# The third weight combination of a chained convolution kernel, with 18 products instead of 19

## The chip, the cores and the metric

The kernel runs on one core of one Trainium2 chip. The metric is the device time of one execution in microseconds (us). TensorE is called PE (its weight loads PEld), VectorE DVE, ScalarE ACT, GpSimd POOL, and SyncE SP. Each engine works through its own queue in the order in which the program issues to it.

## The reference

The input x has 128 samples of 64 channels by 1024 positions. Four layers follow each other, and the result is added to x. Each layer scales a 64x64x3 weight by a style vector of the sample, normalizes it (demodulation), and convolves.

```python
TYPES = ('same', 'upsample', 'same', 'downsample')
def _layer(x, style, w, b, mw, mb, typ):
    s = style @ mw.T + mb
    weight = SCALE * w * s[:, None, :, None]
    demod = lax.rsqrt(jnp.sum(weight * weight, axis=(2, 3)) + EPS)
    weight = weight * demod[:, :, None, None]
    # same: conv; upsample: transposed conv, then blur; downsample: blur, then strided conv
...
x = x + out
```

Nothing nonlinear stands between the layers, so for one sample the whole chain is one linear filter along the positions: nine taps of 64x64 numbers.

## The kernel before, in words

All data are 32-bit floats. The 128 samples are worked on in 32 groups q of four. A group is held as two pairs; a pair has one sample on the upper and one on the lower 64 partitions. Every matmul uses a 64x64 quarter of the PE array, and the four quarters work side by side, so one "product" of a weight with a 64-column block stands in the profile as eight matmul records (two records for each of four quarters).

For each group the kernel first combines the four layers' weights into the nine taps, in three stages, and then filters x with them.

- `stage1_a` and `stage1_b` combine layers 3 and 2 into S (PE into the PSUM buffer psS, ACT evicts psS to S, DVE and POOL finish S). Matmuls L389.
- `stage2` combines S with the blurred layer 1 (E) into the seven blocks of R. Two of its contributions are computed ahead (`share`) and put under its PSUM buffer psR by an ACT copy (`share_copy`, L490). ACT evicts psR to R with two instructions (L545, L360 in the profile). Matmuls L467.
- `stage3` combines R with layer 0 (`woi[0]`) into the nine blocks of W, the third weight combination. In groups 6 to 30 it is split in two. `stage3_b` accumulates twelve products in spare room of a buffer psA, and ACT makes of them two things: four copies psW<-psA of the shared part, and five evicted blocks Wf<-psA. `stage3_a` adds seven products on top of the copies in psW, and ACT evicts four blocks Wf<-psW. Matmuls L571. One POOL instruction (`r_sums`, L588) first adds two pairs of blocks of R, for the shared products.

W is kept with three kinds of taps, and these carry the factors 1, 1/3 and -2. Before the change the factors stand in scaled copies `w0s` of the layer-0 weight, and each kind's three taps lie on their own places (`TAPS`).

The filtering uses five products m = 0..4 of three steps each (`product`, L753, 24 records of 340 columns a product): `conv3`, `conv1`, `conv2` and `conv0` go into psA, `conv4` into the buffer Y. Between them DVE reads psA and prepares what follows: `sum1` (y<-psA,m), `sum2` (two instructions Y<-m,psA, one for each bank of Y, then y<-y,psA). `conv4` adds to Y what it finds there, so it comes after both Y<-m,psA. `combine_a` and `combine_b` (DVE, H<-Wf) make the weights of products 1 to 3. ACT writes the outputs (o<-...), SP loads x and stores the results.

The order is written out by hand (`tc.manual_schedule()`). The loop `turn_of(q)` runs for q = 4 to 28 (25 turns); the first, q = 4, is an `entry` with a slightly different order. With n = q+1, c = q+2, s = q+4, PE's order in a turn is: stage2(c), conv2(q), stage3_b(c), conv4(q), stage3_a(c), conv3(n), stage1_a(s), conv0(q), stage1_b(s), share(c+1), conv1(n). ACT's order is: evict R(c), the psW copies and Wf blocks of stage3_b, the Wf blocks of stage3_a, outputs(q, 2) from Y, evict S(s), copy_m3(n) (m<-psA), outputs(q, 1), share_copy(c+1), outputs(q, 0), scale3. The PSUM buffers psR, psW and psS take turns in the same two banks (pool `ps_w`, one buffer), so each has to be evicted before PE starts the next.

Of the kernel before, what the change touches and what calls it, by code (L numbers as in the profile page):

```python
# [48 lines left out]
F32 = mybir.dt.float32  # L49
# [5 lines left out]
C = 64  # L55
K = 3
# [7 lines left out]
def kernel(  # L64
# [12 lines left out]
    NQ = B // 4  # L77
# [186 lines left out]
    def var_newton(bs, ls=slice(0, NL)):  # L264
# [2 lines left out]


    ALT, ODD, DOWN = slice(0, 4, 2), slice(1, 4, 2), (slice(3, 4), slice(1, 2))
    tA, tB, tBn, tC, t0, t3, td, tb = (  # L270
        const.tile([P, NQ, 2], F32, name=n) for n in ("tA", "tB", "tBn", "tC", "t0", "t3", "td", "tb")
    )

    def table(eng, t, bs, upper, lower, src, mul):
# [24 lines left out]

    def table_0(bs):  # L300
        table(nc_g, t0, bs, ALT, ODD, sc[:, 0, bs], 1.0)


    def table_C(bs, eng=nc_g):
# [81 lines left out]
    def tap_matmul(ps, wd, at, n, weight, taps, first=False, last=False):  # L386
        for r, rows in enumerate(HALF):
            for c, cols in enumerate(HALF):
                nc.tensor.matmul(  # L389
                    ps[r][cols, at * C : (at + n) * C],  # L390
                    weight[rows],
                    wd[c if r == 0 else 1 - c][rows, taps],
                    start=first,
                    stop=last,
                    skip_group_check=True,
                )
# [5 lines left out]
    def flat(t):  # L402
        return t.rearrange("c a o -> c (a o)")
# [18 lines left out]
    def stage1_a(q, ps=None):  # L422

        ps = ps or unit(ps_w, f"psS{q}")
        wd = chain[q]
        tap_matmul(ps, wd, 2, 2, w2n[:, 0, :], EVEN, first=True)
        tap_matmul(ps, wd, 3, 2, w2n[:, 2, :], EVEN)
        tap_matmul(ps, wd, 1, 1, w2n[:, 1, :], slice(1, 2))
        st, t = s_tiles(q)
        for r in range(2):  # L430
            scaled_copy(nc_a, flat(st[r][:, :4]), ps[r][:, C : 5 * C], tBn[:, q, r : r + 1])
        chain[q] = wd, ps, st, t

    def stage1_b(q):

        wd, ps, st, t = chain[q]
        tap_matmul(ps, wd, 2, 1, w2n[:, 3, :], slice(3, 4))
        tap_matmul(ps, wd, 4, 1, w2n[:, 4, :], slice(4, 5), last=True)
        for r in range(2):
            p1 = st[r][:, 0:1, :].to_broadcast([P, 2, C])  # L440
            sums = ps[r][:, 2 * C : 6 * C].rearrange("c (a b o) -> c a b o", a=2, b=2)[:, :, 0]
            nc_v.scalar_tensor_tensor(
                st[r][:, 4:6, :], sums, tB[:, q, r : r + 1], p1, op0=ALU.mult, op1=ALU.subtract
            )
        nc_g.tensor_add(t[:, :, 2], t[:, :, 2], t[:, :, 0])  # L445
        chain[q] = st
        whole[q] = t
# [37 lines left out]
    def share_copy(q):  # L485

        ps = unit(ps_w, f"psR{q}")
        for r in range(2):
            src = shared_ps[q][r].rearrange("c (a o) -> c a o", a=2)
            nc_a.copy(  # L490
                ps[r][:, C : 5 * C].rearrange("c (a b o) -> c a b o", a=2, b=2),
                src[:, :, None, :].to_broadcast([P, 2, 2, C]),
            )
        shared_ps[q] = ps

    def stage2_rest(q):

        ps = shared_ps.pop(q)
        block = lambda i, n=1: [b[:, i * C : (i + n) * C] for b in ps]
        apart = [b[:, : 4 * C].rearrange("c (a b o) -> c a b o", a=2, b=2)[:, :, 0] for b in ps]  # L500
        plan = (
            (apart, E[:, 0], slice(1, 4, 2)),
            (block(1), Ed[:, 0], slice(2, 3)),
            (block(2), Ed[:, 1], slice(1, 2)),
            (block(3), E[:, 2], slice(3, 4)),
            (block(3), Ed[:, 2], slice(2, 3)),
            (block(4), Ed[:, 3], slice(1, 2)),
            (block(4), E[:, 4], slice(3, 4)),
            (block(5, 2), E[:, 8], slice(2, 4)),
            (block(5), E[:, 6], slice(3, 4)),  # L510
            (block(1, 2), E[:, 1], slice(4, 6)),
            (block(2), E[:, 3], slice(4, 5)),
            (block(3), Ed[:, 4], slice(5, 6)),
            (block(4), Ed[:, 5], slice(4, 5)),
            (block(5), E[:, 7], slice(5, 6)),
        )
        for n, (dst, weight, slots) in enumerate(plan):
            chain_matmul(dst, weight, chain[q], slots, n == len(plan) - 1)
        return ps

    def stage2(q, pool=None, engs=(nc_a, nc_a), between=None):
        st = chain[q]
        shared = q in shared_ps
        ps = stage2_rest(q) if shared else unit(pool or ps_w, f"psR{q}")
        for n, e in enumerate(() if shared else (-2, -1, 0, 1, 2, 3, 4, 5, 6)):
            if e % 2 == 0:
                a, lo, m = slice(1, 4), e // 2 + 1, 3
            else:
                a, lo, m = slice(4, 6), (e + 3) // 2, 2
            for r, rows in enumerate(HALF):  # L530
                for c, cols in enumerate(HALF):
                    src = st[c if r == 0 else 1 - c]
                    nc.tensor.matmul(  # L533
                        ps[r][cols, lo * C : (lo + m) * C],
                        E[rows, e + 2, :],
                        src[rows, a, :],
                        start=(n == 0),
                        stop=(n == 8),
                        skip_group_check=True,
                    )  # L540
        if between:
            between()
        t = r_pool.tile([P, 2, 9, C], F32, tag="R", name=f"R{q}")
        for r in range(2):
            scaled_copy(engs[r], flat(t[:, r, :7]), ps[r][:, : 7 * C], tC[:, q, r : r + 1])  # L545
        chain[q] = t
        return ps


    TAPS = slice(3, 9, 2), slice(4, 9, 2), slice(0, 3)  # L550

    def tap(kind, g):
        return range(9)[TAPS[kind]][g]

    def new_w(q):
        Wq[q] = (
# [3 lines left out]

    def tap_shares():
        nc_g.tensor_sub(Wd[:, 0], woi[0][:, 0, :], woi[0][:, 1, :])
        nc_g.tensor_sub(Wd[:, 1], w0s[1][:, 2, :], w0s[1][:, 1, :])

    def blocks(ps, at):
        return [b.rearrange("c (a o) -> c a o", o=C)[:, at, :] for b in ps]
# [10 lines left out]
                    skip_group_check=True,  # L577
                )

    def stage3_out(q, ps, at, n, engs=(nc_a, nc_a)):  # L580
        W = Wq[q][0]
        for r in range(2):
            src = ps[r][:, : n * C].rearrange("c (a o) -> c a o", o=C)
            scaled_copy(engs[r], W[:, at : at + n, r], src, t0[:, q, r : r + 1])

    def r_sums(q, eng):
        t = chain[q]
        eng.tensor_add(t[:, :, 7:9], t[:, :, 2:6:3], t[:, :, 3:7:3])  # L588

    shared_w = {}  # L590

    def stage3_b(q, ps):

        new_w(q)
        t = chain[q]
        plan = (
            (slice(0, 3), w0s[2][:, 2, :], slice(0, 7, 3)),
            (slice(0, 2), w0s[2][:, 1, :], slice(1, 5, 3)),
            (slice(0, 2), w0s[2][:, 0, :], slice(2, 6, 3)),
            (slice(3, 4), w0s[0][:, 0, :], slice(0, 1)),  # L600
            (slice(4, 5), w0s[1][:, 0, :], slice(1, 2)),
            (slice(4, 5), w0s[1][:, 1, :], slice(0, 1)),
            (slice(5, 7), w0s[0][:, 1, :], slice(7, 9)),
        )
        for i, (at, weight, slots) in enumerate(plan):
            same_row(blocks(ps, at), weight, t, slots, i == 0, i == len(plan) - 1)
        pw = shared_w[q] = unit(ps_w, f"psW{q}")
        src = blocks(ps, slice(5, 7))
        for i, f in enumerate((1.0, 1.0 / 3.0)):
            for dst, v in zip(blocks(pw, slice(i, i + 3, 2)), src):  # L610
                scaled_copy(nc_a, dst, v, f)
        stage3_out(q, ps, 0, 5)

    def stage3_a(q):

        t, pw = chain[q], shared_w.pop(q)
        plan = (
            (slice(0, 3, 2), Wd[:, 0], slice(3, 7, 3)),
            (slice(0, 3, 2), w0s[0][:, 2, :], slice(1, 5, 3)),
            (slice(1, 4, 2), Wd[:, 1], slice(2, 6, 3)),  # L620
            (slice(1, 2), w0s[1][:, 0, :], slice(4, 5)),
        )
        for i, (at, weight, slots) in enumerate(plan):
            same_row(blocks(pw, at), weight, t, slots, last=i == len(plan) - 1)
        stage3_out(q, pw, 5, 4)

    def stage3(q, part, pool=None, engs=(nc_a, nc_a)):

# [6 lines left out]
        for i, kind in enumerate(kinds):  # L635
            for k in range(K):
# [11 lines left out]
                    n == 1,  # L648
                    n == K * len(kinds),
                )  # L650
        stage3_out(q, ps, *((3, 6), (0, 3))[part], engs)
        return ps

    def residual(q):
# [592 lines left out]
    def layers(i, j):  # L1247
# [8 lines left out]
        (3, 1): lambda: (table_A(REST, dm[:, 2, REST]), small_rest(3)),  # L1256
        (3, 2): lambda: (
            table_b(PART[1]),
            table_0(REST),
            vector_b1(REST),  # L1260
            vector_c0(REST),
        ),
# [151 lines left out]
    def turn_of(q):  # L1414
# [25 lines left out]
        if entry:  # L1440
            copy_m3(n)
        outputs(q, 2)
        if s < NQ:
            stage1_a(s)
        if not entry:
# [6 lines left out]
        if q in SMALL:  # L1452
            l, bs = SMALL[q]
            nc_v.memset(high(bs.stop - bs.start), 0.0)
        conv0(q, *((2,) if entry else range(K)))
        if entry:
            conv1(n, 0, 1)
        outputs(q, 1)
# [178 lines left out]
```

## Time and profile before

| what | value |
|---|---|
| runs | 479.33, 480.68, 481.21 us; median 480.68 us |
| span of the profiled execution, first to last instruction | 478.0 us (the page gives no other time of it) |
| PE busy | 469.6 us, 98% of the span |
| DVE busy | 417.5 us, 87% |
| ACT busy | 310.1 us, 65% |
| POOL busy | 163.5 us, 34% |
| granted TensorE clock, mean | 0.997 |
| third weight combination, share of the chain that ended last (L571) | 14% (7% into psA, 7% into psW) |

The profile is of one execution. Each row of a timeline gives the start in us, the time from the first start to the last end of a merged run of like instructions, the engine, the line, the operation, the tile written and those read, the shape, and the count; in brackets the idle time of the engine ahead of it and what ended that. Matmuls are pipelined: the end of one overlaps the start of the next, so the pace of PE is read from one start to the next and not from durations, and a PE that is shown as busy can still have waited for part of a microsecond.

### The profile page before, as it was taken

Reading aid. Unit: us, or ns where it says so; the run is one execution under the profiler, and the core shown is the slowest. Engines: PE = TensorE matmul, PEld = TensorE weight load, DVE = VectorE, ACT = ScalarE, POOL = GpSimd, SP = SyncE. Lnnn points to the kernel's source line nnn. Section 1 sums busy time; section 2 is a strip of 40 time slices with the busy share of each in tenths; the row PEclk is TensorE's granted clock in tenths of the full one; section 3 lists DMA queues with packets and bytes.
Section 4 is the critical chain, followed back from the end, with each engine's and each line's share of the span. In section 5 each row is a group of like instructions: output and inputs, shape, how many; then the busy total and the mean of one; then the engine's idle time right before and its main releaser. Section 6 shows DMA issues by size and latency. Waiting matters only on the chain.

```text
span 478.0 us, 26721 instructions
## 1 busy us (share of the span) xinstructions
PE 469.6 (98%) x11928; PEld 346.4 (72%) x11928; DVE 417.5 (87%) x690; ACT 310.1 (65%) x708; POOL 163.5 (34%) x197
## 2 busy tenths in 40 slices
PE   8999999999999999999999999999999999999995
PEld 7877788777878876677776677766887777766652
DVE  5889998879889998899979899979989999999895
ACT  5565666667666676666667666667666768766352
POOL 3434032663335342243432233422434432333200
PEclk9999999999999999999999999999999999999998
DMA  5406365544445554345543455533455554445125
GB/s 175 158 28 200 114 195 192 150 139 144 139 150 157 173 173 127 122 151 160 171 149 120 131 170 152 173 127 126 145 169 162 162 154 146 152 146 170 61 91 191
DMA packets 50514, 70.70 MB, mean 148 GB/s; under 512 B 5664, under 2 KB 47328, under 8 KB 50400
## 3 DMA queue, kind: packets, MB, share of 16 engines
q1 hardware_dynamic: 49808, 68.32, 45.8%
q8 instruction: 93, 1.52, 1.5%
q10 hardware_dynamic: 592, 0.69, 0.5%
q14 instruction: 21, 0.17, 0.1%
HBM read 35.36 MB, written 33.62 MB: 144 GB/s over the span
## 4 chain that ended last, share of the span: by engine, by line
PE 95%; DVE 4%; issue 0%; ACT 0%; ACTq 0%; DVEq 0%
PE psA L753 45%; PE Y L753 11%; PE psR L467 9%; PE psA L571 7%; PE psW L571 7%; PE psS L389 6%; PE psR L533 4%; PE psA L467 2%; PE Y L994 2%; DVE H L662 1%; PE Y L180 1%; PE Y L336 1%; DVE G L662 0%; PE psM L204 0%; DVE o L832 0%
## 5 line engine op out<-in xcount | busy, mean ns | idle before, releaser
L753 PE MATMUL psA<-T,H 64*64 64x340 f32 x2304 | 187.3, 447 | 0.8 <-DVE y L662 0.7
L753 PEld LDWEIGHTS psA<-T,H 64*64 64x64 f32 x2304 | 89.9, 133 | 50.0 <-issue 3.1
L662 DVE SCALAR_TENSOR_TENSOR G<-X 128x1376 f32<-128x1376 f32 (+2 forms) x65 | 78.1, 1207 | 1.1 <-DMA X<-in_x 0.9
L726 POOL TENSOR_TENSOR T<-G 128x684 f32<-128x684 f32 x28 | 46.5, 1659 | 73.1 <-DVE G L662 73.1
L445 POOL TENSOR_TENSOR S<-S 128x128 f32<-128x128 f32 x28 | 22.1, 790 | 144.1 <-ACT S L360 136.8
L360 ACT ACTIVATE R<-psR,tC 128x448 f32<-128x448 f32 x63 | 36.5, 630 | 46.3 <-PE psR L467 26.7
L753 PE MATMUL psA<-T,Wf 64*64 64x340 f32 x768 | 63.9, 446 | 0.0
L753 PE MATMUL Y<-T,Wf 64*64 64x340 f32 x768 | 62.8, 451 | 0.1
L662 DVE SCALAR_TENSOR_TENSOR Y<-m,psA 128x340 f32<-128x340 f32 x64 | 33.1, 517 | 28.0 <-PE psA L753 26.6
L360 ACT ACTIVATE psW<-psA 128x128 f32<-128x128 f32 x100 | 19.3, 269 | 50.3 <-PE psA L571 46.2
L740 DVE TENSOR_TENSOR T<-G 128x1368 f32<-128x1368 f32 (+1 forms) x33 | 50.7, 1540 | 0.0
L360 ACT ACTIVATE Wf<-psW,t 128x256 f32<-128x256 f32 (+2 forms) x76 | 32.7, 479 | 26.5 <-PE psW L571 26.2
L711 DVE TENSOR_TENSOR T<-X 128x684 f32<-128x684 f32 x32 | 47.9, 1496 | 0.0
L467 PE MATMUL psR<-S,E 64*64 64x64 f32 (+1 forms) x1472 | 46.5, 238 | 0.0
L731 POOL TENSOR_TENSOR T<-G 128x684 f32<-128x684 f32 x28 | 46.5, 1660 | 0.0
L389 PEld LDWEIGHTS psS<-wd,w2n 64*64 64x64 f32 x1120 | 35.0, 133 | 13.3 <-ACT S L360 0.8
L467 PEld LDWEIGHTS psR<-S,E 64*64 64x64 f32 x1472 | 39.6, 134 | 5.2 <-ACT psR L490 0.2
L753 PEld LDWEIGHTS Y<-T,Wf 64*64 64x64 f32 x768 | 29.6, 132 | 18.0 <-DVE Y L662 0.7
L830 ACT ACTIVATE o<-psA,tb,td 128x340 f32<-128x340 f32 x63 | 37.0, 647 | 6.3 <-PE psA L753 6.3
L753 PEld LDWEIGHTS psA<-T,Wf 64*64 64x64 f32 x768 | 29.1, 133 | 15.1
L830 ACT ACTIVATE o<-Y,tb,td 128x340 f32<-128x340 f32 x63 | 36.6, 637 | 4.5 <-PE Y L753 2.7
L830 ACT ACTIVATE o<-y,tb,td 128x340 f32<-128x340 f32 x62 | 38.5, 679 | 0.6 <-DVE y L812 0.6
(165 smaller groups left out, 832.4 us busy)
## 6 DMA issues: line engine op xcount, KB each, us to landing
out<-o SPq DMA_DIRECT2D x167, 170.0 KB, 2.6
X<-in_x SPq DMA_DIRECT2D x150, 172.0 KB, 3.6
X<-in_x SPq DMA_DIRECT2D x14, 516.0 KB, 5.3
out<-o SPq DMA_DIRECT2D x6, 510.0 KB, 5.4
out<-o SPq DMA_DIRECT2D x2, 340.0 KB, 3.0
Xe<-in_x_ends SPq DMA_DIRECT2D x1, 512.0 KB, 6.7
out<-o ACTq DMA_DIRECT2D x3, 170.0 KB, 2.3
par<-in_params SPq DMA_DIRECT2D x2, 192.0 KB, 3.4
```

What stands on the lines that cost most here:

```text
L360: nc_a.activation(dst, src, AF.Copy, scale=f)
L389: nc.tensor.matmul(ps[r][cols, at * C : (at + n) * C], weight[rows], wd[c if r == 0 else 1 - c][rows, taps], start=first, stop=last, skip_ ...
L445: nc_g.tensor_add(t[:, :, 2], t[:, :, 2], t[:, :, 0])
L467: nc.tensor.matmul(dst[r][cols], weight[rows], st[c if r == 0 else 1 - c][rows, slots, :], start=False, stop=last, skip_group_check=True,)
L571: nc.tensor.matmul(dst[r][cols], weight[rows], t[rows, c, slots, :], start=first, stop=last, skip_group_check=True,)
L662: nc_v.scalar_tensor_tensor(out, x, f, y, op0=ALU.mult, op1=op)
L711: nc_v.tensor_sub(t[:, pairs, 0, :NJ], plane(X, 3, pairs), plane(X, 1, pairs))
L726: eng.tensor_add(t[:, :, 0, :NJ], plane(g, 2), plane(g, 1))
L731: eng.tensor_sub(t[:, :, 1, :NJ], plane(g, 2), plane(g, 1))
L740: nc_v.tensor_sub(t[:, pairs, :, :NJ], both(a, PL), both(b, 1))
L753: nc.tensor.matmul(ps[s][cols, :NB], w, Ts[q, tag][rows, c, i, g : g + NB], start=(g == 0 and m == 3), stop=(g == K - 1), skip_group_check ...
L830: nc_a.activation(dst, src, AF.Identity, bias=add, scale=d3)
```

## The change

The nine taps are computed with 18 products instead of 19. Three sums of neighbouring blocks of R (0+1, 2+3, 4+5) are multiplied with the middle layer-0 tap, and each result serves two taps: it is copied twice into psW (one ACT copy a bank with a repeated source). `stage3_b` has now six products in four groups (1, 1, 1 and 3 blocks), `stage3_a` twelve in four groups (3, 3, 4 and 2 blocks). The products of taps 0 to 6 use the unscaled weights; their factors 1, 1/3 and -2 come with the eviction, by two further scale tables `t0b` and `t0c`. The taps of a kind lie three apart in W. So ACT evicts two blocks a bank as two instructions after `stage3_b`, and three, two and two blocks a bank as six instructions after `stage3_a`. `r_sums` is two POOL instructions of 192 columns, one for each bank of R, instead of one of 256. The blocks in psR and psS move up by one block of 64 columns, so that block 0 of psW is left untouched until `stage3_a`. In the turn, the first third of conv0(q) moves ahead of stage1_a(s), except in the entry turn; S is evicted ahead of the copy m<-psA in both kernels.

```diff
-        tap_matmul(ps, wd, 2, 2, w2n[:, 0, :], EVEN, first=True)
+        tap_matmul(ps, wd, 3, 2, w2n[:, 0, :], EVEN, first=True)
...
-                ps[r][:, C : 5 * C].rearrange("c (a b o) -> c a b o", a=2, b=2),
+                ps[r][:, 2 * C : 6 * C].rearrange("c (a b o) -> c a b o", a=2, b=2),
...
-    TAPS = slice(3, 9, 2), slice(4, 9, 2), slice(0, 3)
+    TAPS = slice(0, 9, 3), slice(1, 9, 3), slice(2, 9, 3)
...
+    def table_0_kinds():
+        for t, f in ((t0b, 1.0 / 3.0), (t0c, -2.0)):
+            nc_g.tensor_scalar_mul(t, t0, f)
...
     def r_sums(q, eng):
         t = chain[q]
-        eng.tensor_add(t[:, :, 7:9], t[:, :, 2:6:3], t[:, :, 3:7:3])
+        for r in range(2):
+            eng.tensor_add(t[:, r, 7:10], t[:, r, 0:6:2], t[:, r, 1:7:2])
...
     # stage3_b
-            (slice(0, 3), w0s[2][:, 2, :], slice(0, 7, 3)),
-            (slice(0, 2), w0s[2][:, 1, :], slice(1, 5, 3)),
-            (slice(0, 2), w0s[2][:, 0, :], slice(2, 6, 3)),
-            (slice(3, 4), w0s[0][:, 0, :], slice(0, 1)),
-            (slice(4, 5), w0s[1][:, 0, :], slice(1, 2)),
-            (slice(4, 5), w0s[1][:, 1, :], slice(0, 1)),
-            (slice(5, 7), w0s[0][:, 1, :], slice(7, 9)),
+            (slice(3, 4), w0s[1][:, 2, :], slice(5, 6)),
+            (slice(3, 4), w0s[1][:, 1, :], slice(6, 7)),
+            (slice(4, 5), w0s[2][:, 2, :], slice(6, 7)),
+            (slice(0, 3), woi[0][:, 1, :], slice(7, 10)),
...
-        src = blocks(ps, slice(5, 7))
-        for i, f in enumerate((1.0, 1.0 / 3.0)):
-            for dst, v in zip(blocks(pw, slice(i, i + 3, 2)), src):
-                scaled_copy(nc_a, dst, v, f)
-        stage3_out(q, ps, 0, 5)
+        for r in range(2):
+            src = ps[r][:, : K * C].rearrange("c (a o) -> c a o", o=C)
+            dst = pw[r][:, C : 7 * C].rearrange("c (a b o) -> c a b o", b=2, o=C)
+            nc_a.copy(dst, src[:, :, None, :].to_broadcast([P, K, 2, C]))
+        for r, src in enumerate(blocks(ps, slice(3, 5))):
+            scaled_copy(nc_a, Wq[q][0][:, 7:9, r], src, t0[:, q, r : r + 1])
...
     # stage3_a
-            (slice(0, 3, 2), Wd[:, 0], slice(3, 7, 3)),
-            (slice(0, 3, 2), w0s[0][:, 2, :], slice(1, 5, 3)),
-            (slice(1, 4, 2), Wd[:, 1], slice(2, 6, 3)),
-            (slice(1, 2), w0s[1][:, 0, :], slice(4, 5)),
+            (slice(1, 6, 2), Wd[:, 0], slice(1, 6, 2)),
+            (slice(2, 7, 2), Wd[:, 1], slice(0, 5, 2)),
+            (slice(0, 7, 2), woi[0][:, 0, :], slice(0, 7, 2)),
+            (slice(3, 6, 2), woi[0][:, 2, :], slice(1, 4, 2)),
...
-        stage3_out(q, pw, 5, 4)
+        for kind, scale in enumerate((t0, t0b, t0c)):
+            at = slice(kind, 7, K)
+            for r, src in enumerate(blocks(pw, at)):
+                scaled_copy(nc_a, Wq[q][0][:, at, r], src, scale[:, q, r : r + 1])
...
     # turn_of
         outputs(q, 2)
+        if not entry:
+            conv0(q, 0)
         if s < NQ:
             stage1_a(s)
...
-        conv0(q, *((2,) if entry else range(K)))
+        conv0(q, *((2,) if entry else (1, 2)))
```

The blocks of taps 7 and 8 that `stage3_b` evicts with the plain table t0 still get their factors from the scaled weights w0s[1] and w0s[2].

More of the change, by code (lines that the diff above doesn't have):

```diff
@@ L269 @@
     ALT, ODD, DOWN = slice(0, 4, 2), slice(1, 4, 2), (slice(3, 4), slice(1, 2))
-    tA, tB, tBn, tC, t0, t3, td, tb = (
-        const.tile([P, NQ, 2], F32, name=n) for n in ("tA", "tB", "tBn", "tC", "t0", "t3", "td", "tb")
+    tA, tB, tBn, tC, t0, t0b, t0c, t3, td, tb = (
+        const.tile([P, NQ, 2], F32, name=n) for n in ("tA", "tB", "tBn", "tC", "t0", "t0b", "t0c", "t3", "td", "tb")
     )
@@ L425, in stage1_a @@
         wd = chain[q]
-        tap_matmul(ps, wd, 2, 2, w2n[:, 0, :], EVEN, first=True)
-        tap_matmul(ps, wd, 3, 2, w2n[:, 2, :], EVEN)
-        tap_matmul(ps, wd, 1, 1, w2n[:, 1, :], slice(1, 2))
+        tap_matmul(ps, wd, 3, 2, w2n[:, 0, :], EVEN, first=True)
+        tap_matmul(ps, wd, 4, 2, w2n[:, 2, :], EVEN)
+        tap_matmul(ps, wd, 2, 1, w2n[:, 1, :], slice(1, 2))
         st, t = s_tiles(q)
         for r in range(2):
-            scaled_copy(nc_a, flat(st[r][:, :4]), ps[r][:, C : 5 * C], tBn[:, q, r : r + 1])
+            scaled_copy(nc_a, flat(st[r][:, :4]), ps[r][:, 2 * C : 6 * C], tBn[:, q, r : r + 1])
         chain[q] = wd, ps, st, t
@@ L436, in stage1_b @@
         wd, ps, st, t = chain[q]
-        tap_matmul(ps, wd, 2, 1, w2n[:, 3, :], slice(3, 4))
-        tap_matmul(ps, wd, 4, 1, w2n[:, 4, :], slice(4, 5), last=True)
+        tap_matmul(ps, wd, 3, 1, w2n[:, 3, :], slice(3, 4))
+        tap_matmul(ps, wd, 5, 1, w2n[:, 4, :], slice(4, 5), last=True)
         for r in range(2):
             p1 = st[r][:, 0:1, :].to_broadcast([P, 2, C])
-            sums = ps[r][:, 2 * C : 6 * C].rearrange("c (a b o) -> c a b o", a=2, b=2)[:, :, 0]
+            sums = ps[r][:, 3 * C : 7 * C].rearrange("c (a b o) -> c a b o", a=2, b=2)[:, :, 0]
             nc_v.scalar_tensor_tensor(
@@ L498, in stage2_rest @@
         ps = shared_ps.pop(q)
-        block = lambda i, n=1: [b[:, i * C : (i + n) * C] for b in ps]
-        apart = [b[:, : 4 * C].rearrange("c (a b o) -> c a b o", a=2, b=2)[:, :, 0] for b in ps]
+        block = lambda i, n=1: [b[:, (i + 1) * C : (i + 1 + n) * C] for b in ps]
+        apart = [b[:, C : 5 * C].rearrange("c (a b o) -> c a b o", a=2, b=2)[:, :, 0] for b in ps]
         plan = (
@@ L533, in stage2 @@
                     nc.tensor.matmul(
-                        ps[r][cols, lo * C : (lo + m) * C],
+                        ps[r][cols, (lo + 1) * C : (lo + 1 + m) * C],
                         E[rows, e + 2, :],
@@ L542, in stage2 @@
             between()
-        t = r_pool.tile([P, 2, 9, C], F32, tag="R", name=f"R{q}")
+        t = r_pool.tile([P, 2, 10, C], F32, tag="R", name=f"R{q}")
         for r in range(2):
-            scaled_copy(engs[r], flat(t[:, r, :7]), ps[r][:, : 7 * C], tC[:, q, r : r + 1])
+            scaled_copy(engs[r], flat(t[:, r, :7]), ps[r][:, C : 8 * C], tC[:, q, r : r + 1])
         chain[q] = t
         return ps
-    TAPS = slice(3, 9, 2), slice(4, 9, 2), slice(0, 3)
+    TAPS = slice(0, 9, 3), slice(1, 9, 3), slice(2, 9, 3)
     def tap(kind, g):
-        return range(9)[TAPS[kind]][g]
+        return K * g + kind
     def new_w(q):
@@ L562, in tap_shares @@
         nc_g.tensor_sub(Wd[:, 0], woi[0][:, 0, :], woi[0][:, 1, :])
-        nc_g.tensor_sub(Wd[:, 1], w0s[1][:, 2, :], w0s[1][:, 1, :])
+        nc_g.tensor_sub(Wd[:, 1], woi[0][:, 2, :], woi[0][:, 1, :])
     def blocks(ps, at):
@@ L578, in same_row, with w_by_group, stage3_out @@
                 )
-    def stage3_out(q, ps, at, n, engs=(nc_a, nc_a)):
-        W = Wq[q][0]
+    def w_by_group(q, r):
+        return Wq[q][0][:, :, r].rearrange("c (g k) o -> c g k o", k=K)
+    def stage3_out(q, ps, kinds, engs=(nc_a, nc_a)):
         for r in range(2):
-            src = ps[r][:, : n * C].rearrange("c (a o) -> c a o", o=C)
-            scaled_copy(engs[r], W[:, at : at + n, r], src, t0[:, q, r : r + 1])
+            n = len(kinds)
+            src = ps[r][:, : n * K * C].rearrange("c (g k o) -> c g k o", k=n, o=C)
+            dst = w_by_group(q, r)[:, :, kinds[0] : kinds[0] + n]
+            scaled_copy(engs[r], dst, src, t0[:, q, r : r + 1])
     def r_sums(q, eng):
         t = chain[q]
-        eng.tensor_add(t[:, :, 7:9], t[:, :, 2:6:3], t[:, :, 3:7:3])
+        for r in range(2):
+            eng.tensor_add(t[:, r, 7:10], t[:, r, 0:6:2], t[:, r, 1:7:2])
     shared_w = {}
@@ L650, in stage3 @@
                 )
-        stage3_out(q, ps, *((3, 6), (0, 3))[part], engs)
+        stage3_out(q, ps, kinds, engs)
         return ps
@@ L1258 @@
             table_b(PART[1]),
-            table_0(REST),
+            (table_0(REST), table_0_kinds()),
             vector_b1(REST),
```

## The prediction

> **What bounds the kernel now.** I read the page for the engines' shares, the windows view for the length of one ordinary turn, then that turn's timeline engine by engine, because waits below a microsecond show only there.
>
> ```profile
> span 478.0 us, 26721 instructions
> PE 469.6 (98%) x11928; PEld 346.4 (72%) x11928; DVE 417.5 (87%) x690; ACT 310.1 (65%) x708; POOL 163.5 (34%) x197
> PE 95%; DVE 4%; issue 0%; ACT 0%; ACTq 0%; DVEq 0%
> ```
>
> The windows view of the turn (length, then busy time of PE, PEld, DVE, ACT and POOL with counts, the granted clock, DMA):
>
> ```profile
> 378.86:392.70 13.84, 13.84 (x392) 9.81 (x385) 12.88 (x19) 9.85 (x23) 4.83 (x4) 1.00 0.54 160
> ```
>
> PE sets the pace: a turn is 13.84 us of PE work at full clock. Its timeline, from the third weight combination on:
>
> ```profile
> 379.12 0.94 PE L571 MATMUL psA<-R,w0s 64*64 64x192 f32 x24
> 379.88 0.29 PE L571 MATMUL psA<-R,par 64*64 64x64 f32 x8
> 380.00 0.44 PE L571 MATMUL psA<-R,w0s 64*64 64x64 f32 x16
> 380.23 0.42 PE L571 MATMUL psA<-R,par 64*64 64x128 f32 x8
> 380.49 1.95 PE L753 MATMUL Y<-T,Wf 64*64 64x340 f32 x24
> 382.26 0.40 PE L571 MATMUL psW<-R,wsq 64*64 64x128 f32 x8
> ...
> 382.91 0.29 PE L571 MATMUL psW<-R,w0s 64*64 64x64 f32 x8
> 383.03 1.90 PE L753 MATMUL psA<-T,H 64*64 64x340 f32 x24
> 384.74 0.73 PE L389 MATMUL psS<-wd,w2n 64*64 64x128 f32 x24
> 385.29 1.90 PE L753 MATMUL psA<-T,Wf 64*64 64x340 f32 x24
> 387.01 0.41 PE L389 MATMUL psS<-wd,w2n 64*64 64x64 f32 x16
> ...
> 387.59 1.90 PE L753 MATMUL psA<-T,H 64*64 64x340 f32 x24
> 389.31 0.40 PE L467 MATMUL psR<-S,E 64*64 64x128 f32 x8
> ```
>
> From start to start: stage3_b takes 1.37 us (379.12 to 380.49), conv4 1.77, stage3_a 0.77, conv3 1.71, stage1_a 0.55, conv0 1.72, stage1_b with share 0.58, conv1 1.72. A group of eight records costs 0.12 at 64 columns and 0.22 at 128 (382.26 to 382.91 is three such groups), about 0.57 at 340 (a third of 1.71). The first 24 records are one group of 192 and two of 128: 0.76 less 0.44 leaves 0.32 for 192.
>
> PE looks gapless, but conv4 needs Y from DVE, and there the two meet:
>
> ```profile
> 376.74 1.85 DVE L711 TENSOR_TENSOR T<-X 128x684 f32<-128x684 f32 x1
> 379.37 1.07 DVE L662 SCALAR_TENSOR_TENSOR Y<-m,psA 128x340 f32<-128x340 f32 x2 [0.77 <-PE psA L753]
> 407.05 1.07 DVE L662 SCALAR_TENSOR_TENSOR Y<-m,psA 128x340 f32<-128x340 f32 x2 [0.84 <-PE psA L753]
> 408.17 0.52 PE L753 MATMUL Y<-T,Wf 64*64 64x340 f32 x4
> ```
>
> The two Y<-m,psA wait for conv2's last records and end at 379.37+1.07 = 380.44; conv4 starts 0.05 later, at 380.49. Two turns on it is the same: 408.12, then 408.17. Stage3_b's own groups add to 0.76+0.12+0.23+0.22 = 1.33, so it ends at 380.45. The time from conv2's end to conv4 is therefore set by DVE, 1.37 us, and stage3_b just fills it, to within 0.04. At the kernel's end nothing fills it, and PE waits openly:
>
> ```profile
> 468.14 1.07 DVE L662 SCALAR_TENSOR_TENSOR Y<-m,psA 128x340 f32<-128x340 f32 x2
> 469.27 1.95 PE L753 MATMUL Y<-T,Wf 64*64 64x340 f32 x24
> ```
>
> The view of waits says so in a row:
>
> ```profile
> PEld Y L753 <- DVE Y L662: 0.7, 1, 0.7
> ```
>
> Again 468.14+1.07 = 469.21 and conv4 some 0.05 behind.
>
> **Stage3_b loses half its work.** Four groups of 1, 1, 1 and 3 blocks: 3 x 0.12 + 0.32 = 0.68 us instead of 1.33. One product fewer in all, but six leave this place. The 0.65 gained gains nothing: conv4 comes after it on PE and still waits for Y until 1.37 after conv2. Nothing in the change moves sum2 or conv2. Worth 0 in 24 turns; the cover is gone and 0.65 of waiting takes its place. Only in the entry turn, where conv4 is ahead of stage3_b, is the 0.65 real.
>
> **Stage3_a grows.** Groups of 3, 3, 4 and 2 blocks instead of 2, 2, 2 and 1. The 256-column group has no row; between 0.32 (192) and 0.57 (340) it lies at 0.43 on a straight line. So 0.32+0.32+0.43+0.22 = 1.29 against 0.77: +0.52 us. It stands between conv4 and conv3 on PE's path, behind the wait, with nothing to hide it. 24 turns x 0.52 = +12.5 us; entry turn -0.65+0.52 = -0.1.
>
> A rule speaks otherwise. If a group cost by its number of matmuls, stage3_a with four groups before and after would not grow. The Trainium skill, "TensorE: Matmul & The Clock Gate", section "Back-to-back issue gap", gives a sustained 81 ns a matmul at 128 columns and 131 ns at 512, less than twice for four times the width. By an estimate from that page 64, 192 and 256 columns stand at some 73, 89 and 98 ns, the four groups would go from 316 to 357, 13% of 0.77 or +0.1 us, and the sum below would be some 3 us instead of 13. The rows above bear it out poorly: 0.12, 0.22 and 0.57 for 64, 128 and 340 is nearly in proportion.
>
> **GpSimd's sums** are two of 192 columns instead of one of 256. POOL's and ACT's rows of the turn:
>
> ```profile
> 378.94 0.73 POOL L588 TENSOR_TENSOR R<-R 128x256 f32<-128x256 f32 x1 [1.07 <-ACT R L360]
> 377.70 1.16 ACT L360 ACTIVATE R<-psR,tC 128x448 f32<-128x448 f32 x2 [0.71 <-PE psR L467]
> 380.76 0.77 ACT L360 ACTIVATE psW<-psA 128x128 f32<-128x128 f32 x4 [1.90 <-PE psA L571]
> 381.40 0.97 ACT L360 ACTIVATE Wf<-psA,t 128x320 f32<-128x320 f32 x2
> 383.30 0.84 ACT L360 ACTIVATE Wf<-psW,t 128x256 f32<-128x256 f32 x2 [0.93 <-PE psW L571]
> 384.03 1.16 ACT L830 ACTIVATE o<-Y,tb,td 128x340 f32<-128x340 f32 x2
> 385.51 0.84 ACT L360 ACTIVATE S<-psS,tBn 128x256 f32<-128x256 f32 x2 [0.32 <-PE psS L389]
> 386.24 0.72 ACT L792 COPY m<-psA 128x680 f32<-128x680 f32 x1
> 386.84 1.25 ACT L830 ACTIVATE o<-y,tb,td 128x340 f32<-128x340 f32 x2
> 388.15 0.63 ACT L490 COPY psR<-psA 128x256 f32<-128x256 f32 x2
> ```
>
> From the groups by line and shape (count, busy us, mean ns, idle before):
>
> ```profile
> L360 ACT ACTIVATE Wf<-psW,t 128x192 f32<-128x192 f32 x13 | 4.8, 418 | 0.4 <-PE psW L571 0.3 <-PE Y L914 0.2
> ```
>
> A 192-column sum costs at most 0.73 and, at zero fixed cost, 0.55. The first can start when R's first bank is out (about half of the 1.16, 378.3), or, if DVE's T<-X holds it, at 378.59. Two of 0.73 end by 380.05; stage3_b's fourth group then ends at 380.4, still before 380.49. Hidden, even at the upper end; in2, queued behind it on POOL, slips about half a microsecond and is wanted a turn later. If it does hold DVE's H<-Wf back, conv3 has 0.5 us more than before. Two small tables on POOL in turn 3 cost nothing on PE.
>
> **ACT's chain after stage3_a** is where more could be lost. Ahead of it the two psW copies of 384 columns lie between the 0.63 for two of 256 and the 0.72 for one of 680; they run under conv4 and have over a microsecond to spare. After it, two evictions become six: two of 192 columns, four of 128. An instruction's pace is its share of a merged row: 0.84 for two of 256 at some 0.47 each means one every 0.37; 192 columns at 0.418 then one every 0.32. For 128 with a scale table there is no row: 0.17 is the lower bound (psW<-psA, a constant scale), 0.37 the upper; I take 0.27, one more step of 0.05. Six last 2 x 0.32 + 3 x 0.27 + 0.37 = 1.82 (1.4 to 2.2).
>
> On the clock of this turn: stage3_a ends at 382.26+1.29 = 383.55, the evictions run from 383.82 (0.27 later, as now) to 385.64. Stage1_a, which needs psW's banks, is reached at 383.55 + 1.71 (conv3) + 0.57 (the third of conv0 that moves) = 385.83: free. Without that move it would be 385.26 and PE would wait 0.4. Then ACT's two outputs o<-Y (0.52 each) end at 386.7, and S can be evicted from 386.60, exactly when stage1_a is done (385.83+0.55, plus the 0.22 of now). It is out at 387.44; stage1_b, which writes over psS, is reached at 386.38 + 1.15 = 387.53. Then copy, two outputs and share_copy end at 389.71; stage2 comes at 387.53+0.58+1.72 = 389.83. So ACT, idle 0.32 us here now, would have no idle time and PE 0.04 us to spare. One slip costs both places once. At the upper end 0.36 a turn, 8.6 us; at the lower 0. I take 0.05, 1.2 us in all, near the lower end because all shapes but one have rows. S is evicted ahead of the copy m<-psA already now, so that part of the change moves nothing. The higher psR and psS blocks and the strided taps change no count and no size: 0.
>
> **What may come back.** In three turns stage3_b itself is interrupted, with nothing in the profile as the releaser:
>
> ```profile
> 122.11 0.32 PE L571 MATMUL psA<-R,par 64*64 64x128 f32 x1 [0.53 <-issue]
> 193.26 0.45 PE L571 MATMUL psA<-R,w0s 64*64 64x128 f32 x8 [0.32 <-issue]
> 338.78 0.14 PEld L571 LDWEIGHTS psA<-R,par 64*64 64x64 f32 x2 [0.36 <-issue]
> ```
>
> Together 1.2 us that the new wait could swallow; between 0 and -1.2 I take -0.5.
>
> **Sum.** 12.5 - 0.1 + 1.2 - 0.5 = +13.1 us on a span of 478.0: 491.1. The median of the runs lies 2.7 above that span, so 493.8.
>
> **Rivals.**
> - ACT decides (chance 0.09): the evictions take the upper price or more, and S comes late for stage1_b in every turn. 12.5 - 0.1 + 8.6 = +21, 501.7 us. For it: a chain with 0.04 us to spare. Against: the 192-column row, and ACT at 9.85 of 13.84 us. It decides from about 1.9 us for six evictions.
> - The other side, faster (0.05): conv4's start at 0.05 after Y is coincidence, and it really follows stage3_b. Then every one of 25 turns gains 0.65-0.52 = 0.13, 3.2 in all, less 1.2 for ACT: -2.0, 478.7 us; 477.5 where ACT costs nothing. For it: stage3_b does end within 0.04 of Y. Against: the same 0.05 at 469.2, where no stage3_b stands before it. It decides if PE can start conv4 by about 0.55 earlier than Y's second bank.
> - No change (0.04): stage3_a's groups cost by their number; then stage3_b's lost cover alone is left, which costs nothing: 480.7-0.5+1.2, about 481.4 us.
>
> **How the numbers follow.** Forecast 0.82, its own range from 12.4-1.2 = +11.2 less a microsecond of spread between runs, 490.9, to 12.4 and half of ACT's upper price, 497.4. To hold 8 in 10 with part of the ACT rival: 490 to 499. About 0.5% (2.4 us) is what a measurement of this kernel tells from no change. Slower: 0.82+0.09 = 0.91; the coincidence without much of ACT's price is faster, 0.04; the rest, with the no-change case, lies within 0.5%, 0.05.
>
> **What would show it.** Right: the stretch from conv2's end to conv4 stays 1.37 us with PE's records of stage3_b ending some 0.65 before it; stage3_a takes 1.29; an ordinary turn is near 14.4 us; PE waits for DVE Y L662 appear. Wrong: conv4 starting before the second Y<-m,psA ends; stage3_a near 0.8; stage1_b or stage2 waiting for ACT; turns below 13.8.

## The result, and the profile after

The changed kernel takes 492.4 us (492.25 to 492.76, four runs) against 480.0 us for the kernel before beside it (479.02 to 481.21): a ratio of 1.0259, 95% interval 1.0239 to 1.0278. That is 12.4 us slower. The profiled execution has a span of 490.6 us and a time of 492.37 us.

The page of the changed kernel (its line numbers are 5 to 11 higher in the quoted parts: L576 is the third weight combination, L764 the products, L673 the DVE helper, L365 the evictions), then the row of its waits that was not there before, then the windows row of one ordinary turn:

```profile
span 490.6 us, 25623 instructions
PE 476.1 (97%) x11328; PEld 340.8 (69%) x11328; DVE 414.6 (85%) x691; ACT 326.0 (66%) x758; POOL 166.0 (34%) x223
PE 89%; DVE 8%; issue 1%; DMA 1%; ACT 0%; SPq 0%; ACTq 0%; DVEq 0%
```

```profile
PEld Y L764 <- DVE Y L673: 15.8, 25, 0.7
```

```profile
404.11:418.52 14.41, 14.08 (x366) 9.84 (x360) 12.63 (x20) 10.44 (x25) 4.85 (x6) 1.00 0.43 139
```

The chain that ended last now holds 8% of DVE where it held 4%, and PE's weight loads wait 15.8 us for Y, at 25 places, where there was one of 0.7. A turn is 14.41 us against 13.84: 0.57 more. PE's and DVE's rows of a turn, from the third weight combination on:

```profile
403.39 0.53 PE L576 MATMUL psA<-R,w0s 64*64 64x64 f32 x24
403.74 0.69 PE L576 MATMUL psA<-R,par 64*64 64x192 f32 x8
404.76 1.95 PE L764 MATMUL Y<-T,Wf 64*64 64x340 f32 x24 [0.33 <-DVE Y L673]
406.53 0.83 PE L576 MATMUL psW<-R,wsq 64*64 64x192 f32 x16
407.18 0.83 PE L576 MATMUL psW<-R,par 64*64 64x256 f32 x16
407.83 1.90 PE L764 MATMUL psA<-T,H 64*64 64x340 f32 x24
...
409.54 0.75 PE L764 MATMUL psA<-T,Wf 64*64 64x340 f32 x8
410.11 0.73 PE L394 MATMUL psS<-wd,w2n 64*64 64x128 f32 x24
...
412.39 1.94 PE L764 MATMUL psA<-T,H 64*64 64x340 f32 x24
414.15 0.40 PE L472 MATMUL psR<-S,E 64*64 64x128 f32 x8
```

```profile
403.64 1.07 DVE L673 SCALAR_TENSOR_TENSOR Y<-m,psA 128x340 f32<-128x340 f32 x2 [1.04 <-PE psA L764]
```

From conv2's end to conv4 it is 403.39 to 404.76, 1.37 us as before, though the six products now there are done early; the second Y<-m,psA ends at 404.71 and conv4 follows 0.05 later. Stage3_a takes 406.53 to 407.83, 1.30 us instead of 0.77. From conv1 to stage2 it is 1.76 instead of 1.72. These two differences, 0.53 and 0.04, are the 0.57 of the turn. POOL's and ACT's rows:

```profile
402.68 1.14 POOL L598 TENSOR_TENSOR R<-R 128x192 f32<-128x192 f32 x2 [0.81 <-ACT R L365]
```

```profile
404.54 0.85 ACT L618 COPY psW<-psA 128x384 f32<-128x384 f32 x2 [1.41 <-PE psA L576]
405.29 0.64 ACT L365 ACTIVATE Wf<-psA,t 128x128 f32<-128x128 f32 x2
408.10 0.73 ACT L365 ACTIVATE Wf<-psW,t 128x192 f32<-128x192 f32 x2 [2.17 <-PE psW L576]
408.72 0.63 ACT L365 ACTIVATE Wf<-psW,t0b 128x128 f32<-128x128 f32 x2
409.22 0.65 ACT L365 ACTIVATE Wf<-psW,t0c 128x128 f32<-128x128 f32 x2
409.72 1.20 ACT L841 ACTIVATE o<-Y,tb,td 128x340 f32<-128x340 f32 x2
410.88 0.84 ACT L365 ACTIVATE S<-psS,tBn 128x256 f32<-128x256 f32 x2
411.61 0.73 ACT L803 COPY m<-psA 128x680 f32<-128x680 f32 x1
...
413.35 0.65 ACT L495 COPY psR<-psA 128x256 f32<-128x256 f32 x2
```

The sums end at 403.82, well before conv4. The six evictions run from 408.10 to 409.87, 1.77 us; stage1_a starts at 410.11. ACT no longer idles before it evicts S, and its copy under psR ends at 414.00, 0.15 us before stage2.

The 0.04 lies at the start of conv1. Conv1 adds to what conv3 left in psA, so ACT's copy m<-psA has to be out first. That copy ends at 411.61+0.73 = 412.34 and conv1 starts at 412.39, 0.05 later; in the kernel before it ended at 386.96, 0.6 us ahead of conv1. In the trace, conv1's first four records take 0.33 us to the next four instead of 0.29, and all that follows up to stage2 keeps its old pace, so it is conv1 that is held and not stage2.

### The profile page after: what moved, and what is told of

Read it like the earlier page. It is cut to its first block, busy times and chain, and to the rows that moved or that the text cites. A ratio compares the mean times of both kernels' runs of the same rounds, so it can differ in the third digit from the quotient of the medians.

```text
span 490.6 us, 25623 instructions
## 1 busy us (share of the span) xinstructions
PE 476.1 (97%) x11328; PEld 340.8 (69%) x11328; DVE 414.6 (85%) x691; ACT 326.0 (66%) x758; POOL 166.0 (34%) x223
## 4 chain that ended last, share of the span: by engine, by line
PE 89%; DVE 8%; issue 1%; DMA 1%; ACT 0%; SPq 0%; ACTq 0%; DVEq 0%
PE psA L764 44%; PE Y L764 12%; PE psW L576 9%; PE psR L472 9%; PE psS L394 6%; DVE Y L673 5%; PE psR L538 4%; PE psA L472 2%; PE Y L1005 2%; PE psA L576 1%; DMA par_s<-in_params_s 1%; DVE H L673 1%; PE Y L341 1%; DVE G L673 0%; DVE o L843 0%
## 5 line engine op out<-in xcount | busy, mean ns | idle before, releaser
L764 PE MATMUL psA<-T,H 64*64 64x340 f32 x2304 | 187.0, 448 | 0.9 <-DVE y L673 0.7
L764 PEld LDWEIGHTS psA<-T,H 64*64 64x64 f32 x2304 | 88.9, 133 | 51.0 <-issue 2.3
L673 DVE SCALAR_TENSOR_TENSOR G<-X 128x1376 f32<-128x1376 f32 (+2 forms) x65 | 78.1, 1207 | 0.3
L450 POOL TENSOR_TENSOR S<-S 128x128 f32<-128x128 f32 x28 | 12.9, 461 | 167.4 <-ACT S L365 159.8
L764 PE MATMUL Y<-T,Wf 64*64 64x340 f32 x768 | 62.4, 452 | 6.8 <-DVE Y L673 6.6
L764 PE MATMUL psA<-T,Wf 64*64 64x340 f32 x768 | 67.7, 446 | 0.0
L365 ACT ACTIVATE Wf<-psW,t 128x192 f32<-128x192 f32 (+1 forms) x76 | 30.0, 445 | 56.4 <-PE psW L576 55.5
L365 ACT ACTIVATE R<-psR,tC 128x448 f32<-128x448 f32 x63 | 36.6, 631 | 35.5 <-PE psR L472 18.0
L673 DVE SCALAR_TENSOR_TENSOR Y<-m,psA 128x340 f32<-128x340 f32 x64 | 33.1, 516 | 31.4 <-PE psA L764 30.1
L764 PEld LDWEIGHTS Y<-T,Wf 64*64 64x64 f32 x768 | 28.1, 132 | 32.1 <-DVE Y L673 15.8
L722 DVE TENSOR_TENSOR T<-X 128x684 f32<-128x684 f32 x32 | 45.9, 1433 | 0.0
L618 ACT COPY psW<-psA 128x384 f32<-128x384 f32 x50 | 21.2, 467 | 36.7 <-PE psA L576 33.4
L394 PEld LDWEIGHTS psS<-wd,w2n 64*64 64x64 f32 x1120 | 36.0, 133 | 12.4 <-ACT Wf L365 0.5
L764 PEld LDWEIGHTS psA<-T,Wf 64*64 64x64 f32 x768 | 27.9, 133 | 16.1
```

The lines of the kernel that those rows point to most:

```text
L365: nc_a.activation(dst, src, AF.Copy, scale=f)
L394: nc.tensor.matmul(ps[r][cols, at * C : (at + n) * C], weight[rows], wd[c if r == 0 else 1 - c][rows, taps], start=first, stop=last, skip_ ...
L618: nc_a.copy(dst, src[:, :, None, :].to_broadcast([P, K, 2, C]))
L673: nc_v.scalar_tensor_tensor(out, x, f, y, op0=ALU.mult, op1=op)
L722: nc_v.tensor_sub(t[:, pairs, 0, :NJ], plane(X, 3, pairs), plane(X, 1, pairs))
L764: nc.tensor.matmul(ps[s][cols, :NB], w, Ts[q, tag][rows, c, i, g : g + NB], start=(g == 0 and m == 3), stop=(g == K - 1), skip_group_check ...
```

## The experiments

Each kernel was compared with the kernel before on the same chip. Against the changed kernel I compare by the ratios to the kernel before. The stretch ahead of the first conv4 took 31.3 to 35.1 us in the traces here, with no order between the kernels. So the traces are also compared by the time from the first start of conv4 to the last: 438.0 us in the kernel before, 449.7 in the changed kernel, 11.7 more.

**Is it the wait for Y? The sum made shorter, in both kernels.**

```diff
-            for s, a in enumerate(banks(q)):
-                sum_of(Y[:, s, :NB], m3[:, s], 3.0, a[:, :NB])
+            if isinstance(A[q], list):
+                for s, a in enumerate(banks(q)):
+                    sum_of(Y[:, s, :NB], m3[:, s], 3.0, a[:, :NB])
+            else:
+                sum_of(Y[:, :, :NB], m3, 3.0, A[q][:, :, :NB])
```

> The changed kernel with the two instructions Y<-m,psA of 340 columns (1.07 us together) made one of 680 columns over both banks (0.86, the duration of the like-shaped y<-psA,m). Theory, PE waits for Y in every ordinary turn: conv4 comes 0.2 us earlier in 24 turns, 4.9 us less, about 487.5 us. Rival, the added time lies in ScalarE's longer chain, with conv4's wait only slack beside it: no change, 492.4 us.

> The kernel before with the same edit. Theory: there stage3_b's own 1.33 us of products hold conv4 until 0.04 us before Y, so at most 24 x 0.04 = 1.0 us is gained, 479.0 to 480.0 us. If Y's latency bounded the kernel before as well, beyond what the products cover, the same 4.9 us would come, 475 us.

The changed kernel with one sum: 489.44 us, ratio 1.0194 (1.0170 to 1.0218) against 1.0259, some 3 us less. The kernel before with one sum: 477.74 us, ratio 0.9943 (0.9922 to 0.9965). DVE's and PE's rows of the first, then of the second:

```profile
403.12 0.87 DVE L673 SCALAR_TENSOR_TENSOR Y<-m,psA 128x680 f32<-128x680 f32 x1 [1.04 <-PE psA L764]
```

```profile
402.87 0.53 PE L576 MATMUL psA<-R,w0s 64*64 64x64 f32 x24
403.22 0.69 PE L576 MATMUL psA<-R,par 64*64 64x192 f32 x8
404.04 1.37 PE L764 MATMUL Y<-T,Wf 64*64 64x340 f32 x16
```

```profile
378.36 0.87 DVE L662 SCALAR_TENSOR_TENSOR Y<-m,psA 128x680 f32<-128x680 f32 x1 [0.69 <-PE psA L753]
```

```profile
378.09 0.99 PE L571 MATMUL psA<-R,w0s 64*64 64x192 f32 x24
...
379.42 1.94 PE L753 MATMUL Y<-T,Wf 64*64 64x340 f32 x24
381.13 0.45 PE L571 MATMUL psW<-R,wsq 64*64 64x128 f32 x8
```

In the changed kernel conv4 still starts 0.05 us after Y (403.99, 404.04), now 1.17 us after conv2 instead of 1.37: PE follows DVE, as the theory says. In the kernel before Y is now ready at 379.23 and conv4 starts at 379.42, when stage3_b's 1.33 us of products are through: the products hold it.

The gain in the changed kernel is smaller than the 4.9 us expected: its turns are mostly 14.22 us, some 14.3 to 14.6, and from the first conv4 to the last it takes 445.8 us, 3.9 less.

The gain in the kernel before is larger than the 1.0 us at most: from conv4 to conv4 it takes 434.9 us, 3.1 less, and its turn fell from 13.84 to 13.75. Of these 0.09 us, 0.04 lie between conv2 and conv4. The other 0.05 lie in conv4 itself, which takes 1.71 us to stage3_a (379.42 to 381.13) and took 1.77 (380.49 to 382.26). In the ordinary turns of these traces a product that starts behind a wait takes 1.76 to 1.77 us to what follows, as conv1 does in the changed kernel, and one that starts without a wait 1.71 to 1.72. So the 1.77 of conv4 in the kernel before was the mark of a wait already: Y cost it 0.09 us a turn and not 0.04, 2.2 us in 24 turns. The rest of the gain lies in single interrupted turns, which differ between executions. With one sum the kernel before beats both kernels.

**Does the place of a product count, rather than the number? Tap 0 moved from stage3_a to stage3_b.**

```diff
     # stage3_b
+            (slice(5, 6), woi[0][:, 0, :], slice(0, 1)),
...
+        for r, src in enumerate(blocks(ps, slice(5, 6))):
+            scaled_copy(nc_a, Wq[q][0][:, 0:1, r], src, t0[:, q, r : r + 1])
...
     # stage3_a
-            (slice(0, 7, 2), woi[0][:, 0, :], slice(0, 7, 2)),
+            (slice(2, 7, 2), woi[0][:, 0, :], slice(2, 7, 2)),
...
-            at = slice(kind, 7, K)
+            at = slice(kind or K, 7, K)
```

> The changed kernel with the one product of tap 0 (which shares nothing) moved from stage3_a to stage3_b: 7 and 11 products instead of 6 and 12, still 18; tap 0 is evicted by two ACT instructions of 64 columns under conv4. Theory, a product in stage3_b is hidden by the wait for Y and one in stage3_a is not: 24 x 0.11 = 2.6 us less, 489.8 us. Rival, only the number of products counts: 492.4 us.

490.58 us, ratio 1.0219 (1.0198 to 1.0241), 1.8 us under the changed kernel's 492.4 for the same 18 products; the intervals of the two ratios overlap a little, so the times alone would be thin. From conv4 to conv4 it takes 447.4 us, 2.2 less. The rows show the mechanism: conv4 still waits, and stage3_a is 1.19 us (404.22 to 405.41) instead of 1.30.

```profile
402.45 1.95 PE L767 MATMUL Y<-T,Wf 64*64 64x340 f32 x24 [0.33 <-DVE Y L676]
404.22 0.83 PE L576 MATMUL psW<-R,wsq 64*64 64x192 f32 x16
404.87 0.72 PE L576 MATMUL psW<-R,par 64*64 64x192 f32 x16
405.41 1.03 PE L767 MATMUL psA<-T,H 64*64 64x340 f32 x11
```

**Both edits together.**

> The changed kernel with both former edits: one instruction Y<-m,psA and tap 0's product in stage3_b. Theory: both shorten the same wait, from two sides, 14.41 - 0.19 - 0.10 = 14.12 us a turn, 24 x 0.29 = 7.0 us less than the changed kernel, about 485.4 us; 0.35 to 0.4 us a turn of waiting is left, so it stays above the kernel before. Rival, DVE or ScalarE holds the turn once the wait is shorter: 488 us or more.

486.33 us, ratio 1.0122 (1.0101 to 1.0144), 6 us under the changed kernel, and clear of it. From conv4 to conv4 it takes 443.0 us: 6.7 less, where the two edits alone gave 3.9 and 2.2. The two add up, as the theory has it, because the wait is longer than what both take from it. What is left of the wait is in the view of waits, and the kernel is still slower than the one before:

```profile
PEld Y L767 <- DVE Y L676: 11.1, 24, 0.6
```

**What does the moved third of conv0 hide? Moved back, and moved alone in the kernel before.**

```diff
         outputs(q, 2)
-        if not entry:
-            conv0(q, 0)
...
-        conv0(q, *((2,) if entry else (1, 2)))
+        conv0(q, *((2,) if entry else range(K)))
```

> The changed kernel with the first third of conv0 back behind stage1_a. Theory: conv3 ends at 409.54 on the clock of the changed kernel's turn, the last of the six evictions at 409.87, so stage1_a waits 0.38 us for psW's banks in each of 24 turns: 9 us more, 501.5 us. Rival, the move only changes the order of work that fits anyway: 492.4 us.

> The kernel before with the move of conv0's first third ahead of stage1_a, and nothing else of the change. Theory: the order of PE's work alone costs nothing as long as S is out before stage1_b comes 1.14 us after stage1_a, and S's eviction takes 0.22 + 0.84: 480 us, within 1 us. Rival, stage1_b now waits for S: 24 x 0.1 to 0.3, 2 to 7 us more.

Moved back: 501.26 us, ratio 1.0452 (1.0423 to 1.0480), 9 us more than the changed kernel. PE's weight loads wait for the six evictions in 24 turns, half a microsecond each:

```profile
PEld psS L394 <- ACT Wf L365: 12.8, 24, 0.5
```

Alone in the kernel before: 481.14 us, ratio 1.0008 (0.9991 to 1.0024), no difference clear of noise. Its rows do show the small cost that the changed kernel has too, and from conv4 to conv4 it takes 439.0 us, 1.0 more. Conv1 to stage2 takes 1.77 us (405.85 to 407.62), and conv1 starts 0.05 us after ACT's copy m<-psA ends (405.07+0.73 = 405.80).

```profile
405.85 0.50 PE L753 MATMUL psA<-T,H 64*64 64x340 f32 x2
...
407.62 0.42 PE L467 MATMUL psR<-S,E 64*64 64x128 f32 x8
```

```profile
404.34 0.84 ACT L360 ACTIVATE S<-psS,tBn 128x256 f32<-128x256 f32 x2 [0.89 <-PE psS L389]
405.07 0.73 ACT L792 COPY m<-psA 128x680 f32<-128x680 f32 x1
```

**Do the six evictions cost PE anything? Two in their place.**

```diff
-        for kind, scale in enumerate((t0, t0b, t0c)):
-            at = slice(kind, 7, K)
-            for r, src in enumerate(blocks(pw, at)):
-                scaled_copy(nc_a, Wq[q][0][:, at, r], src, scale[:, q, r : r + 1])
+        for r, src in enumerate(blocks(pw, slice(0, 7))):
+            scaled_copy(nc_a, Wq[q][0][:, 0:7, r], src, t0[:, q, r : r + 1])
```

> The changed kernel with two evictions of 448 columns (one a bank, table t0 alone) in place of the six after stage3_a; the factors 1/3 and -2 of the taps 1, 2, 4 and 5 are left out. They take about 1.16 us instead of 1.77. Theory: ScalarE's chain costs PE no more than the 0.04 us a turn by which conv1 to stage2 grew, at most 1.0 us less, 491.4 us. Rival, the six evictions carry a large part of the added time: several us less, down to 480 us.

493.27 us, ratio 1.0264 (1.0238 to 1.0291): nothing gained. ACT's evictions are 1.16 us instead of 1.77, ACT then waits for PE's stage1_a before it evicts S, and conv1 to stage2 still takes 1.76:

```profile
408.33 1.16 ACT L365 ACTIVATE Wf<-psW,t 128x448 f32<-128x448 f32 x2 [2.18 <-PE psW L576]
...
411.11 0.84 ACT L365 ACTIVATE S<-psS,tBn 128x256 f32<-128x256 f32 x2 [0.57 <-PE psS L394]
411.84 0.73 ACT L801 COPY m<-psA 128x680 f32<-128x680 f32 x1
```

```profile
412.62 1.94 PE L762 MATMUL psA<-T,H 64*64 64x340 f32 x24
414.38 0.40 PE L472 MATMUL psR<-S,E 64*64 64x128 f32 x8
```

The copy m<-psA ends at 412.57 and conv1 starts at 412.62, 0.05 later again. So the 0.04 us does not come from the evictions. It stands in the kernel with two evictions and in the kernel before with the move alone, and it belongs to the move: stage1_a, and behind it ACT's S and m<-psA, start a third of conv0 later, while conv1 does not. In the changed kernel with the third moved back, the copy is out 0.33 us before conv1, and conv1 takes 1.72 again.

**Are GpSimd's sums on the path? One sum for both banks.**

```diff
-        for r in range(2):
-            eng.tensor_add(t[:, r, 7:10], t[:, r, 0:6:2], t[:, r, 1:7:2])
+        eng.tensor_add(t[:, :, 7:10], t[:, :, 0:6:2], t[:, :, 1:7:2])
```

> The changed kernel with GpSimd's sums as one instruction for both banks (384 columns, about 1.0 us by the line through 128x256 in 0.73 and 128x684 in 1.66) instead of two by bank. It ends some 0.3 us later, stage3_b's fourth group with it. Theory: that lies in the wait for Y, 0 us, 492.4 us. Rival, the sums are on the path: 24 x 0.3 = 7 us more, 499 us.

493.64 us, ratio 1.0267 (1.0243 to 1.0292): no difference. PE now waits for the sum within stage3_b, and the fourth group still is through before Y is:

```profile
405.95 0.56 PE L576 MATMUL psA<-R,par 64*64 64x192 f32 x8 [0.34 <-POOL R L597]
406.45 1.95 PE L763 MATMUL Y<-T,Wf 64*64 64x340 f32 x24
```

Summing bank by bank buys nothing as long as conv4 waits for Y.

**The wait taken away: conv4 opens Y itself, and DVE adds the sum afterwards, in both kernels.**

```diff
-                        start=(g == 0 and m == 3),
+                        start=(g == 0 and (m == 3 or opens)),
...
+    def sum2_late(q):
+        m3 = late_y[q] = m3c.pop(q)
+        sum_of(m3, m3, 3.0, A[q][:, :, :NB])
...
+    def add_y(q):
+        nc_v.tensor_add(Y[:, :, :NB], Y[:, :, :NB], late_y.pop(q))
...
-            sum2(q)
+            sum2_late(q)
...
             combine_a(n)
-            conv4(q)
+            conv4(q, opens=True)
+            add_y(q)
```

> The changed kernel with conv4's dependence on the sum taken away in the 24 ordinary turns: conv4 opens the buffer Y itself, DVE makes 3*m+psA as one instruction into m (0.86 us) and adds it to Y by a third instruction of 680 columns (about 0.86) after combine_a. The result is the same sum. Theory: stage3_b's end releases conv4, 0.69 us less a turn, 24 x 0.69 = 16.5 us, 476 us, if DVE, at 12.6+0.65 = 13.3 of then 13.7 us a turn, keeps up. Rival, DVE becomes the bound or delays stage1_b's sums: part of it comes back, 480 us or more. If the wait for Y is not what the change exposed: no gain, 492 us or more.

> The kernel before with the same edit. Theory: nothing to gain beyond 24 x 0.04 = 1.0 us, since stage3_b fills the time to Y; DVE's added 0.65 us a turn (12.9 to 13.5 of 13.8) may cost up to some us: 479 to 484 us. If it gains several us, the kernel before was waiting for Y as well.

492.15 us, ratio 1.0238 (1.0217 to 1.0259), nothing gained where the theory had 476 us, and for the kernel before 488.12 us, ratio 1.0156 (1.0129 to 1.0183), more than the 479 to 484 expected. The waits for Y in the ordinary turns are gone, but others took their place: in the first, PE waits for GpSimd's sums and for ACT's copy under psR. The waits, and then the windows rows over the ordinary turns, first of this kernel, then of the changed one:

```profile
PEld psA L576 <- POOL R L598: 7.2, 20, 0.5
PEld psR L472 <- ACT psR L495: 5.6, 16, 0.9
```

```profile
160.00:448.00 288.00, 287.28 (x7137) 219.18 (x7133) 270.87 (x387) 203.71 (x484) 113.81 (x99) 1.00 0.48 146
```

```profile
160.00:448.00 288.00, 282.00 (x7124) 195.38 (x7116) 246.44 (x385) 201.87 (x483) 96.66 (x99) 1.00 0.48 147
```

DVE is busy 94% of the time against 86%. The rival named for this run holds in its number: what the wait gives back, the edit takes elsewhere. The kernel before, which had little to win here, lost some 7.5 us by the same edit, so the edit has a price of its own. The two runs do not separate DVE's additional work from the changed order, for both have both. So they show that conv4 need not wait for Y, but not what 18 products would be worth without that wait. Whether a version with the late sum and a lighter DVE would bring them under the time before was not tried.

## Why the prediction was right

- **The wait for Y that takes stage3_b's place**: right. Conv2's end to conv4 stayed 1.37 us, conv4 0.05 after Y. The waits add to 15.8 us with the 0.7 at the end, 0.63 a turn against 0.65 foreseen. That DVE sets it is shown by the shortened sum. That stage3_b filled the time to within 0.04 is too little: conv4's own pace of 1.77 holds another 0.05. From conv2's end to stage3_a both kernels take 3.14 us, so this changes nothing in the sum.
- **Stage3_a by columns**: right. 1.30 us against 1.29. The 256-column group, which had no row, takes 0.65 less 0.22, 0.43 us, on the straight line. The rule of the Trainium skill that was weighed against the rows ("TensorE: Matmul & The Clock Gate", section "Back-to-back issue gap") would, by the prediction's estimate from it, have given 0.87; the measurement goes with the columns, in the four quarters side by side as they run here.
- **GpSimd's sums hidden**: right, by 1.14 us for two and by the run with one.
- **The moved third of conv0**: its worth was put at 0.4 us a turn, and it measured 9 us in 24 turns.
- **ACT's chain**: the size was near by luck, the place and the cause were wrong. I had 0.05 us a turn from the evictions' pace, 1.2 in all, with S late for stage1_b or the last copy late for stage2. Measured are 0.04 us a turn at the start of conv1, which waits for the copy m<-psA, and from the move of conv0 itself. The six evictions, 1.77 us against 1.82, cost PE nothing.
- **What comes back**: mis-sized. Twenty-four turns of 0.57 less 0.15 in the entry turn would be 13.5 us; between the first and the last conv4 the profiles differ by 11.7 (their starts are 32.27 and 481.94, 449.7 us apart, against 31.29 and 469.27, 438.0 apart). So 1.8 us came back, where I took 0.5 and bounded it by 1.2. Two turns make 1.5 of it: those that end at conv4's starts of 122.12 and 194.10 in the kernel before, where stage3_b was interrupted. I had read the interruptions from the idle time in brackets, 0.53 and 0.32; from conv2's end to conv4 these turns took 2.08 and 1.88 us instead of 1.37. That the new wait swallowed them is not shown: the kernel before with the move alone has no such interruption in these two turns (1.42 and 1.37 us), so the changed kernel's execution may simply have had none there.
- **The sum**: +13.1 us foreseen, 12.4 measured, 11.5 to 13.3 by the interval. In the profiles the spans differ by 12.6, of which 1.0 lies before the first conv4; that stretch varies between executions, so it isn't put to the change. With what they measured the terms come to 11.7: 12.7 for stage3_a and 1.0 for conv1's wait, less 0.15 and 1.8. The times lie nearer to the forecast than these terms do, which is luck within the noise of both.
- **The rivals**: conv4 by coincidence after Y, stage3_a by the number of groups, and ACT as the bound all fell, the first to the two runs with one sum, the second to the row of 1.30, the third to the run with two evictions.

## What to carry to other kernels

Work saved on the bounding engine counts only where that engine isn't about to wait: ask what the removed instructions were hiding, and compare an instruction's start with the end of its producer in the kernel before, for a wait that is just covered looks like no wait at all. Compare also the pace of like products: the one that took 1.77 us beside others of 1.72 was waiting, though no idle time stood before it. When products can be moved between two places, leave them where the wait is; 19 products with twelve in the gap beat 18 with six there. Shortening the producer (one instruction over two banks instead of two) was worth some 3 us in either kernel, moving one product some 2.

## What the runs showed that I had not expected

GpSimd's addition S<-S of 128x128 fell from 790 to 461 ns by its place alone. On the two pages, before and after:

```profile
L445 POOL TENSOR_TENSOR S<-S 128x128 f32<-128x128 f32 x28 | 22.1, 790 | 144.1 <-ACT S L360 136.8
```

```profile
L450 POOL TENSOR_TENSOR S<-S 128x128 f32<-128x128 f32 x28 | 12.9, 461 | 167.4 <-ACT S L365 159.8
```

Before, it began in ordinary turns while DVE ran G<-X, which reads two operands in SBUF; after, S is evicted later and the addition begins when DVE has passed it. The Trainium skill, "SBUF — State Buffer", section "Who interferes with whom", says that a DVE instruction with two SBUF inputs contends with a GpSimd instruction that reads SBUF. The trace before agrees: where the addition began with 0.45 to 1.33 us of G<-X still to run, it ended 0.31 to 0.32 us after G<-X, however long that was. No run took the two apart on purpose, and PE's waits name the addition in neither kernel.
